# Edge counting in a four-layer graph transformer: the check of the totals, the node normalization, the bias rows and a register load change their places

## The chip, the core and the metric

The kernel runs on one core of one Trainium2 chip. The metric is device time in microseconds (us) of one execution. Below, PE is the TensorE matmul engine (PEld its weight loads), DVE is VectorE, ACT is ScalarE, POOL is GpSimd, SP is the queue that starts most transfers. A "q" behind the name (PEldq, DVEq) is the engine's own queue of control instructions.

## What is computed

The reference is one forward pass through four layers on 512 nodes with 768 features. Each layer adds a graph network, a mixture (attention) and a feed-forward network to the nodes. Only the beginning matters here:

```python
xn = _layernorm(x, axis=-1)
x = x + _L0_gnn_ref(xn, edge_index, edge_attr_256, ...) + _L0_mix_ref(xn[None], ...)[0]
...
def _L0_mix_ref(x, qkv_w, qkv_b, proj_w, proj_b, rf):
    qkv = x @ qkv_w.T + qkv_b
    ...
    phi_q = jnp.exp(jnp.einsum('bhnd,md->bhnm', q, rf) - q_norm)
    ...
    return out @ proj_w.T + proj_b
```

There are 8704 edges, with a source, a destination, two type numbers and 256 attributes each. The graph networks need, for each pair of nodes, how many edges of each type join them, and for each node the sum of the attributes of its edges.

## The kernel before

The four layers follow one another in one program of some 39000 instructions. A scheduler puts the instructions of each engine into one fixed order when the program is built: of those that it takes to be ready, the one that stands first in the program goes first. At run time each engine works through its own queue in that order, and an instruction that waits holds up all that is queued behind it. `tc.issue_after(ins)` adds only this: what is written in its block for the engine of `ins` is queued behind `ins`. A tile that lies where an earlier, closed pool lay can be written only when the tiles there have been read for the last time.

**Counting** (`counts`, L431). The edges lie as 128 rows of 68. For each of the 68 columns DVE builds a one-hot matrix of destinations (`ohd`, L510, kept for all 68) and a pair of one-hot matrices of sources, weighted by powers of 256 for the types (`so`, L513, four buffers); PE adds up their products in four PSUM banks (L516). This runs twice, over the lower and the upper 256 source nodes (`h` = 0, 1). Between the columns, every fourth time, the edge attributes of two columns are split into three bf16 parts (L466 to L469, ACT and DVE by turns) and added up over the destinations (L474). After each half, `digits` takes the sums apart: DVE reads the banks (L485), ACT turns bytes into numbers (L488 into `S`, L490 into `R`), POOL and DVE add them up (L492 to L498), ACT and POOL send three results to memory. `S` and `R` have one buffer each, so the second use of `S` waits for the transfer of the first. `eft` holds the attribute sums in two more banks until they are copied to `EFT` (L250, L252). There are eight banks in all (L180).

**The check** (L530 to L544). Type numbers above 2, sums that don't fit, or totals that differ set a flag, `big`. DVE reduces the totals, PE adds them over the partitions (a 128 x 128 matrix of ones by `check`), and DVE makes the flag from it. It is written at the end of `counts`.

**Nodes.** `norm` (L391 to L406) takes statistics (L402, L403) and a root (L404, L405) for each of four blocks of 128 nodes and scales them into `xn` (L406). It is queued behind column 34 of the second half (`begun`). `to_fm` (L357) turns `xn` with 24 transposes on PE (L355) into six banks, and six copies bring them into `xnT` (DVE and ACT by turns). `xn` and `xnT` are in pools opened behind `counts`, on the memory of the counting.

**First mixture** (`mix0`, L644). `tm` (L319) multiplies `xnT` by the weights of the values in eight groups of twelve matmuls and a thirteenth that adds the bias; then come two groups of four heads, and `project`, which turns the result and multiplies it by the output weights, again with a bias row. `bias` (L280) fetches one row of 768 numbers with POOL's queue and splits it into three bf16 parts with five POOL instructions: three copies (L291, L293, L295) and two subtractions (L292, L294).

**Branches.** Behind the mixture each of the five engines loads the flag into a register (L2089) and takes a branch (L2090); with a flag of 0 the longer counting is skipped. The third layer does the same again (L1560, L1561).

Of the kernel before, what the change touches and what calls it, by code (L numbers as in the profile page):

```python
# [10 lines left out]
F32 = mybir.dt.float32  # L11
BF16 = mybir.dt.bfloat16
# [4 lines left out]
OP = mybir.AluOpType  # L17
# [4 lines left out]
P = 128  # L22
N = 512
NT = N // P
D = 768
KC = D // P
HW = 384
NE = 8704
EJ = NE // P
# [141 lines left out]
class Net:  # L171
    def __init__(self, ctx, tc, dram, at, out):
# [43 lines left out]
        nc.gpsimd.iota(self.me, pattern=[[0, 1]], base=0, channel_multiplier=1, allow_small_or_imprecise_dtypes=True)  # L216
        self.identb = keep.tile([P, P], BF16, name="identb")
        self.big0 = keep.tile([P, 1], F32, name="big0")
        nc.gpsimd.memset(self.big0, -BIG)
# [211 lines left out]
    def counts(self, c0, g0):  # L431
# [10 lines left out]
        AT = g0.tile([P, NT, N], F32, name="AT")  # L442
        after = c0.enter_context(tc.tile_pool(name="g0_t", bufs=1))
        EFT = after.tile([P, 2, N], F32, name="EFT")
        with ExitStack() as c:
# [10 lines left out]

            top = one.tile([P, 8], F32, name="top")
            total = one.tile([P, 10], F32, name="total")

# [19 lines left out]
            def digits(h, t, ps):  # L479
# [8 lines left out]
                nc.scalar.copy(S[:, :3, :], held[0])  # L488
                R = dg.tile([P, 3, N], F32, name="R", bufs=1)
                nc.scalar.copy(R, held[1])  # L490
                R16 = dg.tile([P, 3, N], I16, name="R16", bufs=1)
                nc.gpsimd.tensor_copy(R16, R)  # L492
                nc.gpsimd.tensor_add(A, R[:, 0, :], R[:, 1, :])
                nc.vector.scalar_tensor_tensor(A, A, 0.0, R[:, 2, :], OP.add, OP.add, accum_out=total[:, k : k + 1])
# [11 lines left out]
            for h in range(2):  # L506
# [15 lines left out]
                for t in range(2):  # L522
                    digits(h, t, [acc[t, n] for n in range(2)])

                while len(left) > (17, 0)[h]:
                    features(left.pop(0))
            for f in range(2):
                self.copy(EFT[:, f, :], eft[f])

            three = one.tile([P, EJ], F32, name="three")  # L530
            nc.vector.tensor_scalar(three, ind[:, 3, :], 2.0, None, OP.is_le, OP.add, accum_out=total[:, 8:9])
            nc.vector.tensor_scalar(total[:, 8:9], total[:, 8:9], -1.0, float(-EJ), OP.mult, OP.add)
            nc.vector.memset(total[:, 9:10], 0.0)
            check = one.tile([P, 2], F32, name="check")
            nc.vector.tensor_reduce(check[:, 0:1], total, AX.X, OP.add)
            high = one.tile([P, 1], F32, name="high")
            nc.vector.tensor_reduce(high, top, AX.X, OP.max)
            nc.vector.tensor_scalar(check[:, 1:2], high, 2.0 ** 24, None, OP.is_ge)
            p = self.ps()
            self.acc(p[:, :2], [(self.ones, check)])  # L540
            bad = one.tile([P, 2], F32, name="bad")
            nc.vector.tensor_scalar(bad, p[:, :2], 0.0, None, OP.not_equal)
            nc.vector.tensor_reduce(high, bad, AX.X, OP.max)
            nc.vector.tensor_copy(self.big, high)  # L544
        return AT, EFT, after

# [96 lines left out]

    def mix0(self, xnT):  # L644
        nc, tc, d = self.nc, self.tc, self.d
        scale = 96 ** -0.5
        xs = self.chunks(xnT)
        with ExitStack() as outer, ExitStack() as c:
# [15 lines left out]

            self.tm(d["m0_wqkv"], xs, put_v, self.bias(d["m0_bv"]), nbs=(4, 5), bias_at=2 * D)
            for g in range(2):
                qk = one.tile([97, 2, 4, N], F32, name="qk")
                for s, b in ((0, "m0_bq"), (1, "m0_bk")):
# [47 lines left out]
            c.close()  # L716
            self.project(outer, attn, "m0")

# [840 lines left out]
    def gnn2(self, xn, xnT):  # L1559
        big = self.nc.values_load(self.big[:1], min_val=0, max_val=1)  # L1560
        with self.tc.If(big > 0) as cmp:  # L1561
            self.gnn2_with(xn, xnT, False)
        with cmp.Else():
            self.gnn2_with(xn, xnT, True)
# [497 lines left out]
def tile_net(ctx, tc, dram, at, out, only=ALL):  # L2062
# [10 lines left out]
    with ExitStack() as ck, ExitStack() as c0:  # L2073
        g0 = c0.enter_context(tc.tile_pool(name="g0", bufs=1))
        if "counts" in only:
            AT, EFT, g0_t = net.counts(c0, g0)
        nodesT = ck.enter_context(tc.tile_pool(name="L0k", bufs=1, side="right")).tile([P, KC, N], F32, name="nodesT")
        with tc.tile_pool(name="L0", bufs=1) as pool:
            xnT = pool.tile([P, KC, N], F32, name="xnT")
            with tc.tile_pool(name="L0n", bufs=1) as p2:  # L2080
                xn = p2.tile([P, NT, D], F32, name="xn")
                with tc.issue_after(net.begun[0]), tc.issue_after(net.begun[1]):
                    net.constants()
                    net.norm(net.x, xn)
                net.to_fm(xn, xnT)
            if "mix0" in only:
                net.mix0(xnT)
            if "gnn0" in only:
                wrong = nc.values_load(net.big[:1], min_val=0, max_val=1)  # L2089
                with tc.If(wrong > 0):  # L2090
                    net.counts_any(AT)
                with ExitStack() as e:
                    net.gnn0(nodesT, xnT, AT, net.degrees(e, g0_t, AT, EFT))
        c0.close()
        if "gnn0" in only:
            net.attention0(nodesT)
# [62 lines left out]
```

## Time and profile before

| | us |
|---|---|
| median of three runs (4174.07 to 4178.53) | 4176.57 |
| the profiled execution | 4179.75 |
| its span | 4177.7 |
| PE busy | 4027.0 (96%) |
| first matmul of the counting | 13.24 |
| end of the first half's matmuls of columns | about 119 |
| first matmul of the second half | 127.5 |
| flag written (L544) | 246.2 |
| first matmul of the mixture's values | 252.36 |
| first matmul behind the branch | 489.63 |

A row of the timeline reads: start and duration in us, engine, line, operation, what is written <- what is read, shape, number of instructions merged, and in brackets the idle time of the engine before it with what ended it. A row of the waits reads: who waited <- for what, then total us, number of times, longest. "Granted clock" is the share of full speed at which TensorE was let run in a stretch. All spans come from one profiled execution.

### The profile page before, as it was taken

How to read it: one execution, taken by the hardware profiler on the slowest of the kernel's cores; microseconds unless marked ns; L12 is line 12 of the kernel's file. 1: busy time of each engine (PE TensorE's matmuls, PEld its weight loads, DVE VectorE, ACT ScalarE, POOL GpSimd, SP SyncE). 2: the span in 40 equal slices, each digit the busy share in tenths (PEclk: the TensorE clock that was granted, in tenths of full speed). 3: DMA queues.
4: the chain of work that ended last, by engine and by line, in shares of the span. 5: the costliest groups of instructions: out<-in, count | busy, mean ns of one | idle time of the engine just before them, and what ended most of it. 6: DMA issues, size and time to landing. Idle time of an engine off the chain costs nothing. (4 is left out here: it accounts for less than half of the span.)

```text
span 4177.7 us, 39229 instructions
## 1 busy us (share of the span) xinstructions
PE 4027.0 (96%) x16020; PEld 2066.7 (49%) x16061; DVE 1214.8 (29%) x2899; ACT 648.5 (16%) x1222; POOL 274.4 (7%) x329
## 2 busy tenths in 40 slices
PE   8989999999999999999999999999989999999998
PEld 3444555554455667655544444454644444444443
DVE  7721211113332147313411111126832122212211
ACT  1212000012222216311101010024510000000000
POOL 1120000010031010000000000020200000000000
PEclk9999999999999999999999999999999999999999
DMA  3210011121184011302211111082099999999998
GB/s 124 71 69 34 35 63 51 53 78 36 62 312 143 23 70 46 132 25 78 98 46 57 46 61 42 3 325 82 15 373 422 421 421 421 421 422 421 422 422 361
DMA packets 99548, 710.89 MB, mean 170 GB/s; under 512 B 12608, under 2 KB 12944, under 8 KB 29984
## 3 DMA queue, kind: packets, MB, share of 16 engines
q1 hardware_dynamic: 78064, 601.20, 36.0%
q0 software_dynamic: 16816, 95.80, 6.1%
q10 hardware_dynamic: 4480, 11.28, 0.7%
q8 instruction: 131, 2.15, 0.2%
q14 instruction: 57, 0.47, 0.0%
HBM read 685.68 MB, written 22.54 MB: 170 GB/s over the span
## 5 line engine op out<-in xcount | busy, mean ns | idle before, releaser
L1981 PE MATMUL ps<-w,xg 128*64 128x384 f32 x3072 | 567.6, 489 | 5.3 <-DMA w<-in_f_Wg_dram 3.0
L1981 PEld LDWEIGHTS ps<-w,xg 128*64 128x64 f32 x3072 | 235.3, 137 | 293.1 <-issue 264.1
L1601 PE MATMUL ps<-aT,w 128*128 128x512 f32 x864 | 372.3, 592 | 0.0
L1997 PE MATMUL ps<-w,hT 128*64 128x384 f32 x1536 | 322.5, 490 | 6.3 <-DMA w<-in_f_Wd_dram 2.9
L334 PE MATMUL ps<-xnT,w 128*128 128x512 f32 (+1 forms) x732 | 322.8, 598 | 0.2 <-ACT xnT L252 0.2
L1601 PEld LDWEIGHTS ps<-aT,w 128*128 128x128 f32 x864 | 164.2, 190 | 203.6 <-issue 202.3
L334 PE MATMUL ps<-w,xnT 128*128 128x384 f32 x672 | 222.7, 488 | 0.0
L334 PEld LDWEIGHTS ps<-xnT,w 128*128 128x128 f32 (+1 forms) x732 | 134.7, 185 | 176.3 <-issue 172.7
L1997 PEld LDWEIGHTS ps<-w,hT 128*64 128x64 f32 x1536 | 132.5, 136 | 171.8 <-issue 146.5
L411 DVE TENSOR_TENSOR x<-x,ps 128x384 f32<-128x384 f32 x224 | 123.4, 553 | 263.7 <-PE ps L334 193.0
L334 PE MATMUL ps<-C,parts 128*128 128x512 bf16 x843 | 187.8, 380 | 3.5 <-DVE inv L1623 2.4
L334 PE MATMUL ps<-w,hT 128*128 128x384 f32 x552 | 184.6, 490 | 2.6 <-ACTq L1056 1.7
L334 PEld LDWEIGHTS ps<-w,xnT 128*128 128x128 f32 x672 | 127.7, 191 | 88.8 <-issue 5.8
L1611 DVE TENSOR_TENSOR aT<-inv,ps 128x512 f32<-128x512 f32 x72 | 49.4, 686 | 365.7 <-PE ps L334 365.7
L1984 ACT ACTIVATE h<-ps 128x384 f32<-128x384 f32 x64 | 31.4, 490 | 788.9 <-PE ps L1981 788.9
L516 PE MATMUL ps<-ohd,so 128*128 128x512 bf16 x533 | 128.4, 391 | 21.1 <-DVE so L513 20.4
L1985 DVE TENSOR_TENSOR h<-h,ps 128x384 f32<-128x384 f32 x64 | 35.4, 554 | 376.8 <-PE ps L1981 376.8
L334 PEld LDWEIGHTS ps<-w,hT 128*128 128x128 f32 x552 | 103.1, 190 | 80.1 <-ACT xbT L252 7.1
L334 PE MATMUL ps<-w,aT 128*128 128x384 f32 (+1 forms) x416 | 139.6, 486 | 0.5 <-DVE aT L250 0.4
L334 PE MATMUL ps<-xnT,sw 128*128 128x512 f32 x288 | 139.6, 616 | 0.0
L334 PEld LDWEIGHTS <-parts 128*128 128x128 bf16 x864 | 84.8, 98 | 108.1 <-issue 8.9
L334 PE MATMUL ps<-w,nodesT 128*128 128x384 f32 x384 | 129.1, 486 | 0.0
(507 smaller groups left out, 4634.7 us busy)
## 6 DMA issues: line engine op xcount, KB each, us to landing
w<-in_f_Wg_dram SPq DMA_DIRECT2D x128, 1152.0 KB, 22.2
w<-in_f_Wu_dram SPq DMA_DIRECT2D x128, 1152.0 KB, 22.2
w<-in_f_Wd_dram SPq DMA_DIRECT2D x128, 1152.0 KB, 22.2
w<-in_g_w_dram SPq DMA_DIRECT2D x54, 1152.0 KB, 5.2
w<-in_m_wqkv_dram SPq DMA_DIRECT2D x24, 1152.0 KB, 7.5
w<-in_g_t_dram SPq DMA_DIRECT2D x12, 1152.0 KB, 5.1
w<-in_m_wp_dram SPq DMA_DIRECT2D x8, 1152.0 KB, 5.1
ea<-in_edge_attr_dram SPq DMA_DIRECT2D x34, 256.0 KB, 2.7
```

Source lines behind the costliest of these rows:

```text
L334: i = self.nc.tensor.matmul(out, a, b, start=n == 0, stop=n == len(pairs) - 1)
L411: self.nc.vector.tensor_add(xs, xs, p)
L516: nc.tensor.matmul(p, so[:, n, t * P : (t + 1) * P], ohd[:, j, :], start=j == 0, stop=j == EJ - 1)
L1601: nc.tensor.matmul(outs[nb * 3 + f], w[:, k, f * P : (f + 1) * P], xT[:, k, :], start=first and k == 0, stop=last and k == KC - 1)
L1611: nc.vector.tensor_mul(aT[:, f, :], inv[:, r, :], p)
L1981: nc.tensor.matmul(p[a * 64 : a * 64 + 64, :HW], xg[:, k, a * CAP : (a + 1) * CAP], ws[b][a][:, k, :], start=k == 0, stop=k == KC - 1)
L1984: nc.scalar.activation(h, pg[:, :HW], AF.Silu)
L1985: nc.vector.tensor_mul(h, h, pu[:, :HW])
L1997: nc.tensor.matmul(po[nb][a * 64 : a * 64 + 64, :HW], hT[:, f * P + a * 64 : f * P + a * 64 + 64], wd[a][:, f, nb * HW : (nb + 1) * HW], s ...
```

## The change

Six things are altered.

- The small tiles of the check move into one long-lived tile, `edge`. The check itself becomes a function, `checked`, that `mix0` calls behind the products of the values. The counting of type numbers (L531 to L533) is queued behind column 34 of the second half.
- `xn` is allocated before the counting, on the right side of the memory, in a place of its own; normalization is otherwise queued as before. `nodesT` takes that place once `xn` has been turned. `EFT` is allocated behind the counting instead of before it.
- `R` is bf16 instead of f32.
- The bias row of the values and all of POOL's work in `project` are queued behind the last POOL sum of counts of the first half (`self.after`, L493 with `t` = 1). At the start of the program they were free to go at once.
- The flag is loaded once, ahead of the second group of heads, and both branches use that register.
- The third layer's load is dropped.

```diff
--- before.py
+++ after.py
@@ -215,6 +215,7 @@
         self.me = keep.tile([P, 1], F32, name="me")
         nc.gpsimd.iota(self.me, pattern=[[0, 1]], base=0, channel_multiplier=1, allow_small_or_imprecise_dtypes=True)
         self.identb = keep.tile([P, P], BF16, name="identb")
+        self.edge = keep.tile([P, 24], F32, name="edge")
         self.big0 = keep.tile([P, 1], F32, name="big0")
         nc.gpsimd.memset(self.big0, -BIG)
         self.wq1 = keep.tile([P, KC, 32], F32, name="wq1")
@@ -440,8 +441,6 @@
         self.S32 = self.dp.tile([NT, P, 4, N], F32, name="S32")
         self.big = self.keep.tile([P, 1], I32, name="big")
         AT = g0.tile([P, NT, N], F32, name="AT")
-        after = c0.enter_context(tc.tile_pool(name="g0_t", bufs=1))
-        EFT = after.tile([P, 2, N], F32, name="EFT")
         with ExitStack() as c:
             one = c.enter_context(tc.tile_pool(name="c_one", bufs=1))
             ep = c.enter_context(tc.tile_pool(name="c_e", bufs=2))
@@ -454,8 +453,7 @@
             attr = d["edge_attr_256"].rearrange("(p j) f -> p j f", p=P)
             eft = [self.ps() for _ in range(2)]
 
-            top = one.tile([P, 8], F32, name="top")
-            total = one.tile([P, 10], F32, name="total")
+            top, total, check, high, bad = (self.edge[:, a:b] for a, b in ((0, 8), (8, 18), (18, 20), (20, 21), (21, 23)))
 
             def features(q):
 
@@ -486,11 +484,12 @@
                     held.append(whole.bitcast(U8).rearrange("p (n b) -> p b n", b=4)[:, :3, :])
                 S = dg.tile([P, 4, N], F32, name="S", bufs=1)
                 nc.scalar.copy(S[:, :3, :], held[0])
-                R = dg.tile([P, 3, N], F32, name="R", bufs=1)
+
+                R = dg.tile([P, 3, N], BF16, name="R", bufs=1)
                 nc.scalar.copy(R, held[1])
                 R16 = dg.tile([P, 3, N], I16, name="R16", bufs=1)
                 nc.gpsimd.tensor_copy(R16, R)
-                nc.gpsimd.tensor_add(A, R[:, 0, :], R[:, 1, :])
+                made["add"] = nc.gpsimd.tensor_add(A, R[:, 0, :], R[:, 1, :])
                 nc.vector.scalar_tensor_tensor(A, A, 0.0, R[:, 2, :], OP.add, OP.add, accum_out=total[:, k : k + 1])
                 nc.gpsimd.tensor_add(S[:, 3, :], S[:, 0, :], S[:, 1, :])
                 nc.vector.scalar_tensor_tensor(S[:, 3, :], S[:, 3, :], 0.0, S[:, 2, :], OP.add, OP.add,
@@ -521,28 +520,34 @@
                         self.begun = made["so"].ins, made["part"].ins
                 for t in range(2):
                     digits(h, t, [acc[t, n] for n in range(2)])
+                if h == 0:
+                    self.after = made["add"].ins
 
                 while len(left) > (17, 0)[h]:
                     features(left.pop(0))
-            for f in range(2):
-                self.copy(EFT[:, f, :], eft[f])
 
             three = one.tile([P, EJ], F32, name="three")
-            nc.vector.tensor_scalar(three, ind[:, 3, :], 2.0, None, OP.is_le, OP.add, accum_out=total[:, 8:9])
-            nc.vector.tensor_scalar(total[:, 8:9], total[:, 8:9], -1.0, float(-EJ), OP.mult, OP.add)
-            nc.vector.memset(total[:, 9:10], 0.0)
-            check = one.tile([P, 2], F32, name="check")
+            with tc.issue_after(self.begun[0]):
+                nc.vector.tensor_scalar(three, ind[:, 3, :], 2.0, None, OP.is_le, OP.add, accum_out=total[:, 8:9])
+                nc.vector.tensor_scalar(total[:, 8:9], total[:, 8:9], -1.0, float(-EJ), OP.mult, OP.add)
+                nc.vector.memset(total[:, 9:10], 0.0)
+        after = c0.enter_context(tc.tile_pool(name="g0_t", bufs=1))
+        EFT = after.tile([P, 2, N], F32, name="EFT")
+        for f in range(2):
+            self.copy(EFT[:, f, :], eft[f])
+
+        def checked():
+
             nc.vector.tensor_reduce(check[:, 0:1], total, AX.X, OP.add)
-            high = one.tile([P, 1], F32, name="high")
             nc.vector.tensor_reduce(high, top, AX.X, OP.max)
             nc.vector.tensor_scalar(check[:, 1:2], high, 2.0 ** 24, None, OP.is_ge)
             p = self.ps()
             self.acc(p[:, :2], [(self.ones, check)])
-            bad = one.tile([P, 2], F32, name="bad")
             nc.vector.tensor_scalar(bad, p[:, :2], 0.0, None, OP.not_equal)
             nc.vector.tensor_reduce(high, bad, AX.X, OP.max)
             nc.vector.tensor_copy(self.big, high)
-        return AT, EFT, after
+
+        return AT, EFT, after, checked
 
     def counts_any(self, AT):
 
@@ -641,7 +646,7 @@
         return EFP
 
 
-    def mix0(self, xnT):
+    def mix0(self, xnT, checked):
         nc, tc, d = self.nc, self.tc, self.d
         scale = 96 ** -0.5
         xs = self.chunks(xnT)
@@ -662,8 +667,13 @@
                 h = (nb - 4) * 4
                 self.copy(v[:, t, h : h + 4, :96], p.rearrange("p (h d) -> p h d", h=4))
 
-            self.tm(d["m0_wqkv"], xs, put_v, self.bias(d["m0_bv"]), nbs=(4, 5), bias_at=2 * D)
+            with tc.issue_after(self.after):
+                bv = self.bias(d["m0_bv"])
+            self.tm(d["m0_wqkv"], xs, put_v, bv, nbs=(4, 5), bias_at=2 * D)
+            checked()
             for g in range(2):
+                if g:
+                    self.wrong = nc.values_load(self.big[:1], min_val=0, max_val=1)
                 qk = one.tile([97, 2, 4, N], F32, name="qk")
                 for s, b in ((0, "m0_bq"), (1, "m0_bk")):
                     w = self.wk(d["m0_wqkv"][2 * s + g, 0])
@@ -714,7 +724,8 @@
                     nc.vector.tensor_mul(attn[:, :, hh * 96 : (hh + 1) * 96], p[:, :, :96],
                                          r.to_broadcast([P, NT, 96]))
             c.close()
-            self.project(outer, attn, "m0")
+            with tc.issue_after(self.after):
+                self.project(outer, attn, "m0")
 
     def project(self, c, attn, m, done=None):
 
@@ -1557,8 +1568,7 @@
             self.project(c, attn, "m2")
 
     def gnn2(self, xn, xnT):
-        big = self.nc.values_load(self.big[:1], min_val=0, max_val=1)
-        with self.tc.If(big > 0) as cmp:
+        with self.tc.If(self.wrong > 0) as cmp:
             self.gnn2_with(xn, xnT, False)
         with cmp.Else():
             self.gnn2_with(xn, xnT, True)
@@ -2073,21 +2083,21 @@
     with ExitStack() as ck, ExitStack() as c0:
         g0 = c0.enter_context(tc.tile_pool(name="g0", bufs=1))
         if "counts" in only:
-            AT, EFT, g0_t = net.counts(c0, g0)
-        nodesT = ck.enter_context(tc.tile_pool(name="L0k", bufs=1, side="right")).tile([P, KC, N], F32, name="nodesT")
+            right = ExitStack()
+            xn = right.enter_context(tc.tile_pool(name="L0n", bufs=1, side="right")).tile([P, NT, D], F32, name="xn")
+            AT, EFT, g0_t, checked = net.counts(c0, g0)
+            with tc.issue_after(net.begun[0]), tc.issue_after(net.begun[1]):
+                net.constants()
+                net.norm(net.x, xn)
         with tc.tile_pool(name="L0", bufs=1) as pool:
             xnT = pool.tile([P, KC, N], F32, name="xnT")
-            with tc.tile_pool(name="L0n", bufs=1) as p2:
-                xn = p2.tile([P, NT, D], F32, name="xn")
-                with tc.issue_after(net.begun[0]), tc.issue_after(net.begun[1]):
-                    net.constants()
-                    net.norm(net.x, xn)
-                net.to_fm(xn, xnT)
+            net.to_fm(xn, xnT)
+            right.close()
+            nodesT = ck.enter_context(tc.tile_pool(name="L0k", bufs=1, side="right")).tile([P, KC, N], F32, name="nodesT")
             if "mix0" in only:
-                net.mix0(xnT)
+                net.mix0(xnT, checked)
             if "gnn0" in only:
-                wrong = nc.values_load(net.big[:1], min_val=0, max_val=1)
-                with tc.If(wrong > 0):
+                with tc.If(net.wrong > 0):
                     net.counts_any(AT)
                 with ExitStack() as e:
                     net.gnn0(nodesT, xnT, AT, net.degrees(e, g0_t, AT, EFT))
```

## The prediction

> **What bounds the kernel now.** I read the busy shares first. TensorE (PE) is busy 96% of a span of 4177.7 us, so a change pays only where PE stands still or runs at a low clock. The edit touches the counting of the edges and the first mixture, all before 500 us. Next I read the waits of PE from 0 to 560 us.
>
> ```profile
> PE ps L516 <- DVE so L513: 20.4, 8, 13.2
> PE ps L334 <- DVE check L535: 7.8, 1, 7.8
> PE ps L334 <- DVEq L2090: 6.2, 1, 6.2
> ...
> PE ps L474 <- ACT part L468: 2.9, 2, 2.2
> ```
>
> Columns: total us, times, longest. The first row holds 13.2 us of start-up; the remaining 7.2 us are short of one-hot pairs (`so`) at the start and between the two halves of the counting. The second is the test of the totals, the third the branch behind the mixture. Then the timeline of PE at the start, and of DVE and POOL beside it.
>
> ```profile
> 13.24 3.90 PE L516 MATMUL ps<-ohd,so 128*128 128x512 bf16 x9 [13.24 <-DVE so L513]
> 17.53 0.82 PE L516 MATMUL ps<-ohd,so 128*128 128x512 bf16 x3 [0.38 <-DVE so L513]
> 19.94 0.40 PE L516 MATMUL ps<-ohd,so 128*128 128x512 bf16 x1 [1.59 <-DVE so L513]
> 21.64 3.17 PE L516 MATMUL ps<-ohd,so 128*128 128x512 bf16 x7 [1.30 <-DVE so L513]
> 26.57 8.10 PE L516 MATMUL ps<-ohd,so 128*128 128x512 bf16 x28 [1.76 <-DVE so L513]
> ```
>
> ```profile
> 14.97 2.50 DVE L513 TENSOR_SCALAR so<-io,ind,worth 128x256 bf16<-128x256 int16 x2
> 14.98 1.63 POOL L292 TENSOR_TENSOR row<-row,bias 1x768 f32<-1x768 f32 x1
> ```
>
> Nine matmuls in 3.90 us are 0.43 each; the three at 17.53 take 0.27. So PE comes up to its full clock after about 3.9 us of unbroken work, loses it in the gaps (granted clock 0.50 from 20 to 30 us), and has it again at 30.4. The gaps come from DVE: the same pair of `so` takes 0.59 us at 12.85 and 2.50 at 14.97, while POOL splits bias rows. Last, the end of the counting:
>
> ```profile
> 235.54 1.90 PE L474 MATMUL ps<-ohd,part 128*128 128x512 bf16 x7 [1.21 <-DVE part L469]
> 245.25 0.56 PE L334 MATMUL ps<-check,ones 128*128 128x2 f32 x2 [7.81 <-DVE check L535]
> 247.24 5.27 PE L355 MATMUL ps<-ident,xn 128*128 128x128 f32 x24 [1.43 <-DVE xn L406]
> 252.36 4.11 PE L334 MATMUL ps<-w,xnT 128*128 128x384 f32 x12
> ```
>
> PE ends the edge features at about 237.3, waits for the check, then for the normalized nodes, turns them at half clock (0.50 from 242 to 252) and starts the mixture's values at 252.36: 15.1 us.
>
> **The change, part by part.**
>
> *Bias rows away from the start.* Two rows, `m0_bv` and `m0_bp`, cost POOL three copies of 0.81 and two subtractions of 1.63 each: 5.69 a row, 11.4 us, from 13.99 to 26.43. In that time (14.13 to 25.63) DVE finished twelve operations worth 0.26 each, 3.1 us of work in 11.5: 27%. It isn't the DMA traffic: the DMA engines were full already at 12.6 to 14.0, where `ohd` took its normal 0.34. Without the rows DVE makes one edge column in 0.26 + 2 x 0.26 = 0.78 us; PE uses one in 4 x 0.226 = 0.90 (sixteen matmuls in 3.62 us at full clock) or 1.72 cold. So PE is never starved after 13.24: nine cold matmuls to 17.14, then 39 at 0.226 = 8.8, so the first feature group, which starts at 34.51 now, starts at 26.0. **-8.5**. Bounds: -5.0, the gaps alone (0.38 + 1.59 + 1.30 + 1.76), and -9. I take -8.5, since the three matmuls at 17.53 were at full clock.
>
> *The rows in their new place.* They are queued on POOL behind the last sum of counts of the first half (L493, now at 131.3) and ahead of, or among, L495, L498 and three transfers of the digits; their two row fetches (0.53 each to issue) go with them, and the rows of the first graph layer, fetched at 22 and 26 now, come after. Queued behind POOL are DVE's L496, which waits for L495, and every `so` behind that. The same 11.4 us of POOL now lie at about 136 to 150. DVE loses 73% of them, 8.3 us. It is what PE waits for until 141; afterwards it stands idle 2.5 us of each 6.05:
>
> ```profile
> 146.15 0.69 DVE L467 TENSOR_TENSOR ea<-ea,part 128x512 f32<-128x512 f32 x1 [2.50 <-ACT part L466]
> ```
>
> Two such pauses give back 5.0, so 3.3 stay. **+3.3**, bounds 0 (four `so` buffers cover it) and +8.3 (nothing does). Here a rule of the Trainium skill speaks against the change: SBUF — State Buffer (the summary of port contention) says that DVE in its two-port modes and GpSimd hold a port pair in turn, each blocking the other for a whole instruction. By the rule alone moving a row moves its whole block: 11.4 away, 11.4 back, nothing won. The rows say DVE does get 27% through, and that the price depends on DVE's slack at the place: 8.5 where it has none and the clock is cold, 3.3 where it idles 41%.
>
> *Nodes normalized beside the counting.* Statistics and roots already run at 174 to 183; only the four scalings (L406, 2.52 us) waited, as their tile lay in memory that the counting held. On the other side of SBUF they can run at 183. The DVE queue holds `so` behind them; DVE idles 2.5 of the next 6 us and features are prepared one group ahead. **0**; without that cover +2.5. Below nothing: no, DVE work is only added there.
>
> *The end of the counting.* The check leaves the path, and with `xn` ready the 24 transposes follow the features at 237.3. At full clock the same step is in the trace at the mixture's end:
>
> ```profile
> 447.53 2.97 PE L355 MATMUL ps<-ident,attn 128*128 128x128 f32 x24
> 450.91 4.14 PE L334 MATMUL ps<-w,aT 128*128 128x384 f32 x12 [0.41 <-DVE aT L250]
> ```
>
> 3.4 us from first transpose to next projection. They need six PSUM banks: two are free in the second half, and four are read out by L485 until 231.7. The copies to `xnT` share DVE and ACT with the last digits: I add 0.6, one such operation. The values start at 241.3 instead of 252.36. **-11.1**. Bounds: -8, if the copies queue behind L488 and L500, which wait for the digits' transfer and end at 243.4; -13, if transposes fill PE's two gaps of 1.9 us at 233 to 236. The clock: TensorE: Matmul & The Clock Gate (the HAM part) has the gate close after one idle window of about 3.4 us. By that alone PE, only half busy from 232 to 238, might meet the transposes cold: 5.27 instead of 2.97, -8.8. The row gives 1.00 until 242, 4.7 us after PE stopped, and 1.00 through the similar gaps at 132 to 142. I use the row.
>
> *The check inside the mixture.* Its three DVE steps, one product, and three DVE steps (0.15 each) go behind the values. On PE it costs 0.56 for two passes cold, about half warm: **+0.3** (bounds 0 and 1). DVE waits for PE mostly there (7.5 us at a time). The counting of types (L531 to L533) moves off DVE's start, which waits for a transfer at that point: 0.
>
> *bf16 digits.* R shrinks; ACT writes it, POOL and DVE read it. The nearest rows, POOL's copies of one row from f32 and from bf16, both take 0.81: 0, bounds -1 and +2 (four sums of 1.3 us).
>
> *One register load.* Each engine now loads the flag at the second head group, about 366 us. On PE's queue it takes 0.487 at 477.8 while matmuls go on to 483.5, so it hides behind queued matmuls (2.03 us of them before 366): 0, bounds 0 and +1.5. What waits behind it: PE's next projection, ACT's exponentials, DVE's scalings. SP's load must wait for the flag at about 275; the projection's weights may queue behind it and are used at 440. At the branch, DVE's load of 0.55 (483.5) goes and the branch itself stays: **-0.5** (0 to -0.6). The later loads, at 2033 on PE, made nobody wait: 0.
>
> Sum: -8.5 + 3.3 + 0 - 11.1 + 0.3 - 0.5 = -16.5. The profiled execution took 4179.75 us (2.05 more than its span); it would take 4163.3. The runs shown have a median of 4176.57, 3.2 lower, so: **4160**. Everything behind 500 us, the last stage's weight stream included, shifts as a whole.
>
> **Rivals.**
> *The covers hold too well or the rows cost nothing:* transposes fill the gaps, DVE hides the rows: -8.5 - 13 - 0.2 = -21.7, 4155.
> *The rows cost all that DVE loses:* -8.5 + 8.3 - 11.1 - 0.2 = -11.5, 4165. For it: DVE is behind when they come. Against: the pauses at 144 and 150.
> *The rows do not thin out the start, or the copies queue behind the digits:* the scheduler orders DVE anew and the start stays starved (-11.1 + 3.3 - 0.2 = -8), or the full loss and late copies together (-8.5 + 8.3 - 8 - 0.2 = -8.4): 4168.5, near to no change.
> *DVE's queue stands in the middle (slower):* L496 is queued ahead of the pairs, at 133, and POOL splits both rows before L495. The row fetches land as late as the first did (7.5 us from issue to first use), at 141; then 11.4 of rows and 1.5 of L495: DVE stands until 154, 21 us, PE runs dry and restarts cold (half of 3.9 us, 1.9): +22.9 in place of +3.3, a sum of +3.1, 4180. It decides from 20 us on. Against it: L496 comes late in DVE's queue now (138.93), behind five pairs, and the same order should follow POOL's new one.
>
> **How the numbers follow.** Forecast (4156 to 4164) 0.52; covers too good 0.13; full price 0.14; near no change 0.14; slower 0.07. A measurement here can't tell less than 0.2%, 8.4 us. Faster by over that: the first three nearly whole, 0.77; slower by over that: the tail of the last, 0.03; between, 0.20. The range 4153 to 4170 takes in the fourth case and leaves out the slower one and the far end of the second.
>
> **What would show it.** First feature group near 26; PE without gaps at 17 to 27. POOL's row steps (L291 to L295) behind the first half's digits, and DVE's pairs slow beside them; PE's waits for `so` there up by 3. L406 before 190. Transposes near 232 in 3.0 us (all is 5.2 earlier by then: -8.5 + 3.3), values 4 us after their start. The branch's wait 5.7. It would be wrong if the row steps fell beside another late DVE stretch, or if the transposes waited for a place, a bank or the clock.

## The result and the profile after

The changed kernel took 4162.06 us (median of nine runs, 4156.76 to 4168.25), the kernel before 4178.16 on the same chip (nine runs, 4174.07 to 4181.6): ratio 0.9962, 95% interval 0.9952 to 0.9972, 16.1 us less. The forecast was 4160 from a median of 4176.57, a step of 16.5. The terms of the sum did not all come out so well: the rows cost half of what was forecast in their new place, the register load won nothing, and a loss of 3.1 us stood in no term.

The profiled execution took 4156.76 us for a span of 4154.5. The views of before are taken up in their order. The waits of PE from 0 to 560 us (who waited <- for what: total us, times, longest):

```profile
PE ps L515 <- DVE so L512: 15.4, 5, 11.9
PE ps L335 <- DVEq L2100: 6.5, 1, 6.5
...
PE ps L472 <- ACT part L466: 2.8, 2, 1.7
```

The wait of 7.8 us for the check is gone. The wait for one-hot pairs is down by 5.0, the branch's wait is there as before. The timeline of PE and of DVE at the start:

```profile
11.94 13.08 PE L515 MATMUL ps<-ohd,so 128*128 128x512 bf16 x48 [11.94 <-DVE so L512]
24.86 2.75 PE L472 MATMUL ps<-ohd,part 128*128 128x512 bf16 x12
```

```profile
15.95 0.60 DVE L512 TENSOR_SCALAR so<-io,ind,worth 128x256 bf16<-128x256 int16 x2
```

48 matmuls run without a break, and a pair of `so` takes 0.60 us at about the time at which it took 2.50 before. The first group of edge attributes starts at 24.86; the forecast said 26.0. Behind the first half's digits PE waited for pairs before, too (first fence); now POOL's row steps lie there, and the waits are longer (second fence, PE and then DVE beside it):

```profile
133.49 3.27 PE L516 MATMUL ps<-ohd,so 128*128 128x512 bf16 x12 [0.55 <-DVE so L513]
138.04 2.76 PE L516 MATMUL ps<-ohd,so 128*128 128x512 bf16 x12 [1.28 <-DVE so L513]
```

```profile
128.15 4.44 PE L515 MATMUL ps<-ohd,so 128*128 128x512 bf16 x19 [1.34 <-DVE so L512]
139.55 0.82 PE L515 MATMUL ps<-ohd,so 128*128 128x512 bf16 x3 [1.31 <-DVE so L512]
130.16 9.34 DVE L512 TENSOR_SCALAR so<-io,ind,worth 128x256 bf16<-128x256 int16 x10
```

The end of the counting, on PE:

```profile
227.68 1.90 PE L472 MATMUL ps<-ohd,part 128*128 128x512 bf16 x8 [0.21 <-DVE part L467]
229.42 2.78 PE L356 MATMUL ps<-ident,xn 128*128 128x128 f32 x24
232.49 4.11 PE L335 MATMUL ps<-w,xnT 128*128 128x384 f32 x12 [0.29 <-ACT xnT L253]
```

The transposes follow the last attributes with nothing between, at full clock (2.78 us for 24), and the values start at 232.49 instead of 252.36.

All comparisons below use three distances, all between first matmuls on PE: *start* (first column to first group of attributes), *half 2* (last group of attributes in the first half to last group in the second), *tail* (from there to the mixture's values). The changed kernel was profiled twice (experiment 10), and the two executions differ in their clock.

| kernel | first matmul | start | half 2 | tail | values start | median us (before on that chip) |
|---|---|---|---|---|---|---|
| before | 13.24 | 21.27 | 108.15 | 25.09 | 252.36 | |
| changed | 11.94 | 12.92 | 109.87 | 13.15 | 232.49 | 4162.06 (4178.16) |
| changed, second profile | 11.98 | 13.05 | 109.82 | 13.14 | 232.60 | 4163.53 (4177.14) |
| rows early | 12.12 | 22.02 | 107.93 | 12.97 | 239.64 | 4166.59 (4174.07) |
| rows only | 13.06 | 11.96 | 110.05 | 25.29 | 244.97 | 4166.86 (4174.07) |
| check first | 12.21 | 12.35 | 109.81 | 23.54 | 242.52 | 4167.05 (4174.07) |
| nodes late | 12.87 | 13.20 | 109.82 | 18.15 | 238.64 | 4161.64 (4174.07) |
| `edge` 64 wide | 11.43 | 12.25 | 109.82 | 14.69 | 232.79 | 4158.84 (4176.66) |
| pad in before | 11.68 | 20.82 | 108.15 | 25.11 | 250.37 | 4179.33 (4176.66) |
| rows in an idle place | 12.00 | 12.46 | 110.14 | 15.12 | 234.32 | 4161.74 (4176.66) |
| two loads | 13.01 | 12.43 | 109.85 | 14.82 | 234.72 | 4162.59 (4176.66) |
| rows spread | 11.96 | 12.59 | 108.57 | 13.13 | 230.85 | 4158.28 (4177.14) |

The medians of one kernel before differ by up to 4 us between chips, so a median is read against the one in brackets beside it.

### The profile page after: what moved, and what is told of

Read it like the earlier page. It is cut to its first block, busy times and chain, and to the rows that moved or that the text cites. A ratio compares the mean times of both kernels' runs of the same rounds, so it can differ in the third digit from the quotient of the medians.

```text
span 4154.5 us, 39257 instructions
## 1 busy us (share of the span) xinstructions
PE 4020.7 (97%) x16061; PEld 2061.7 (50%) x16061; DVE 1212.8 (29%) x2899; ACT 648.6 (16%) x1222; POOL 273.4 (7%) x329
```

## The experiments

**1. Rows early.** The changed kernel with the bias rows free to go at once, as they were.

```
-            with tc.issue_after(self.after):
-                bv = self.bias(d["m0_bv"])
+            bv = self.bias(d["m0_bv"])
...
-            with tc.issue_after(self.after):
-                self.project(outer, attn, "m0")
+            self.project(outer, attn, "m0")
```

> The changed kernel with both bias rows free to go at the start again, as before the change; all else as changed. Theory (POOL's row steps starve DVE at the start, and cost less behind the first half's digits): the first feature group is back near 33 to 34.5 us instead of 24.9, the step between the halves is as short as in the kernel before, the tail is as short as in the changed kernel; values of the mixture start near 240 (before 252.4, changed 232.5), total about 12 us below the kernel before and 6 to 8 above the changed one. Rival (the transfers, not POOL, starve DVE at the start): first feature group stays near 25 and the total equals the changed kernel's.

Measured 4166.59, ratio 0.9982 (0.9973 to 0.9991). PE at the start:

```profile
22.98 1.89 PE L515 MATMUL ps<-ohd,so 128*128 128x512 bf16 x4 [2.21 <-DVE so L512]
...
34.14 2.75 PE L472 MATMUL ps<-ohd,part 128*128 128x512 bf16 x11
```

The gaps are back and the attributes start at 34.14, with everything else of the change in place: POOL's row steps, and nothing else that was altered, thinned the start. (Their two small fetches move with them; experiment 7 has the same thinning with the DMA engines 14% busy.) Between the halves this kernel takes 107.93, as before (108.15). Its matrix of normalized nodes is made within that stretch (179.3 to 186.8), so the four scalings cost nothing there. The total missed its expectation: 7.5 us below the kernel before instead of 12. The values do start 12.7 earlier, but 3.2 of that is lost in the last stage (experiments 5 and 6) and 1.1 is the first matmul's, which no part of the change explains.

**2. Rows only.** The kernel before with that one part of the change.

```
-                nc.gpsimd.tensor_add(A, R[:, 0, :], R[:, 1, :])
+                made["add"] = nc.gpsimd.tensor_add(A, R[:, 0, :], R[:, 1, :])
...
+                if h == 0:
+                    self.after = made["add"].ins
...
+            with tc.issue_after(self.after):
+                bv = self.bias(d["m0_bv"])
...
+            with tc.issue_after(self.after):
+                self.project(outer, attn, "m0")
```

> The kernel before with nothing changed but the place of the two bias rows. Theory: first feature group near 25 to 26, between the halves 2 to 3.5 us lost again, tail of 15.1 us as before: values start near 244.5 to 247, total 5 to 8 us below the kernel before. Rival (a move of the rows wins nothing, since their whole block comes back): total within 2 us of the kernel before, with PE's waits for pairs between the halves up by 8.

Measured 4166.86, ratio 0.9984 (0.9977 to 0.9991): 7.2 us less, where experiment 1, all but this part, gave 7.5 less. Start 11.96, 9.3 shorter; between the halves 110.05, 1.9 longer; tail unchanged. So the rows are worth 8 to 9 at the start and cost about 2 where they go.

**3. Check first.** The changed kernel, with the transposes held behind the check; the nodes are still ready early.

```
-            self.acc(p[:, :2], [(self.ones, check)])
+            self.checking = self.acc(p[:, :2], [(self.ones, check)]).ins
...
-            checked()
...
-            net.to_fm(xn, xnT)
+            checked()
+            with tc.issue_after(net.checking):
+                net.to_fm(xn, xnT)
```

> The changed kernel with the check called right behind the counting, and the transposes queued behind its product on PE. Theory (the wait for the check was most of the tail, and cost the clock as well): PE stands about 8 us for the check, the transposes take 5.3 us at half clock instead of 2.8, values start about 10.5 us later than in the changed kernel (243), total up by 10 to 11 against it. Rival (nodes ready early is what counted, the check would be hidden by it): values start within 3 us of the changed kernel's.

Measured 4167.05, ratio 0.9986 (0.9979 to 0.9992). PE at the end of the counting:

```profile
237.09 0.56 PE L335 MATMUL ps<-edge,ones 128*128 128x2 f32 x2 [6.70 <-DVE edge L541]
237.50 4.78 PE L356 MATMUL ps<-ident,xn 128*128 128x128 f32 x24
242.52 4.14 PE L335 MATMUL ps<-w,xnT 128*128 128x384 f32 x12 [0.24 <-DVE xnT L251]
```

The tail is 23.54. Ready nodes alone are worth only 1.6 of the 11.9 us: PE waits 6.70 for the totals, and then turns the nodes at about half speed, 4.78 instead of 2.78.

**4. Nodes late.** The changed kernel, with `xn` back in the memory of the counting and the check left in the mixture.

```
-            right = ExitStack()
-            xn = right.enter_context(tc.tile_pool(name="L0n", bufs=1, side="right")).tile([P, NT, D], F32, name="xn")
...
-            net.to_fm(xn, xnT)
-            right.close()
...
+            with tc.tile_pool(name="L0n", bufs=1) as p2:
+                xn = p2.tile([P, NT, D], F32, name="xn")
+                with tc.issue_after(net.begun[0]), tc.issue_after(net.begun[1]):
+                    net.constants()
+                    net.norm(net.x, xn)
+                net.to_fm(xn, xnT)
```

> The changed kernel with the normalized nodes back in the memory that the counting gives free; the check stays in the mixture. Theory: the four scalings start only behind the last feature matmul, transposes begin 0.7 to 1.5 us later and keep full clock; values start 1 to 2.5 us later than in the changed kernel, total up by as much. Rival (the own place was the larger part): values start 5 us later or more.

Measured 4161.64, ratio 0.9970 (0.9958 to 0.9982); tail 18.15, 6.9 shorter than before. The three views are PE, DVE and POOL at the end of the counting:

```profile
234.09 4.26 PE L356 MATMUL ps<-ident,xn 128*128 128x128 f32 x24 [3.37 <-DVE xn L407]
```

```profile
231.37 4.41 DVE L407 TENSOR_SCALAR xn<-x,mv,rs 128x768 f32<-128x768 f32 x4
```

```profile
230.93 1.48 POOL L491 CAST R<-R 128x1536 int16<-128x1536 bf16 x1
232.36 1.16 POOL L492 TENSOR_TENSOR AT<-R 128x512 f32<-128x512 bf16 x1
```

The expectation missed: the tail is 5.0 longer than the changed kernel's, not 1 to 2.5, and the transposes did not keep full clock. The four scalings took 4.41 us here and 2.52 in the kernel before: they now lie beside POOL's digits, the same collision as at the start. Moving the check alone gives 6.9, early nodes alone 1.6, both 11.9. The two parts are worth 3.4 more together than one by one: each alone leaves PE a wait (6.70 or 3.37), and behind it slow transposes (4.78 or 4.26).

**5 and 6. The tile `edge`.** The profile of the changed kernel showed a loss that no step of the forecast had: from the first down product of the last stage to the end 1080.4 us, where the kernel before and experiment 2 have 1077.3. Experiments 1, 3 and 4 are as slow (1080.3 to 1080.5). What all the slower ones have and the other two have not includes `edge`, 96 bytes per partition that live to the end; every tile allocated behind it, the weight buffers included, lies 96 bytes further on. Experiment 5 gives it 256 bytes in the changed kernel; experiment 6 adds 96 bytes to the kernel before, and changes nothing else.

```
-        self.edge = keep.tile([P, 24], F32, name="edge")
+        self.edge = keep.tile([P, 64], F32, name="edge")
```

```
+        pad = keep.tile([P, 24], F32, name="pad")
+        nc.gpsimd.memset(pad, 0.0)
```

> The changed kernel with the long-lived tile of the check 256 bytes wide instead of 96, so that all that lies behind it in SBUF stands where it stood before, modulo 256. Theory (the 96 bytes shift the last stage's weight buffers off a 256-byte boundary, and each 9216-byte piece of a transfer then takes 351 ns instead of 349): pieces back at 349 ns, rate back at 422 GB/s, from the first down product of the last stage (near 3070) to the end 1077.3 us as before instead of 1080.4, total 3 us below the changed kernel, near 4159. Rival (the last stage is longer for its later or earlier start or the missing register load): still 1080.4, 351 ns.

> The kernel before with an unused long-lived tile of 96 bytes and nothing else. Theory: pieces of 9216 bytes take 351 ns, the last stage 1080.4 us instead of 1077.3, values start as before (252), total 3 us above the kernel before. Rival: no change.

Measured 4158.84, ratio 0.9957 (0.9944 to 0.9971), and 4179.33, ratio 1.0007 (0.9999 to 1.0015). The last stage took 1077.1 in the first and 1080.4 in the second, and the pieces of 9216 bytes took 349 and 351 ns. Medians alone would not settle it, as the interval of experiment 6 just touches 1; the windows from 3700 to 3900 us do, in the order before, changed, experiment 5, experiment 6. The columns are the window, its length, busy time (and number) of PE, PEld, DVE, ACT and POOL, granted clock, DMA share and, last, GB/s.

```profile
3700.00:3900.00 200.00, 199.38 (x1034) 89.34 (x1032) 38.24 (x102) 11.95 (x24) 4.24 (x7) 1.00 1.01 422
```

```profile
3700.00:3900.00 200.00, 197.81 (x999) 87.22 (x996) 45.26 (x129) 11.47 (x23) 4.24 (x7) 1.00 1.01 420
```

```profile
3700.00:3900.00 200.00, 199.28 (x1017) 88.38 (x1014) 44.14 (x126) 11.50 (x23) 4.24 (x7) 1.00 1.01 421
```

```profile
3700.00:3900.00 200.00, 198.53 (x1022) 88.42 (x1018) 39.42 (x108) 11.98 (x24) 4.24 (x7) 1.00 1.01 420
```

The DMA engines are full in all four, and with the 96 bytes they move less. The waits of PE in the last stage (3070 to the end) show whom it reaches, first before, then changed:

```profile
PE ps L1981 <- DMA w<-in_f_Wg_dram: 3.0, 2, 1.5
PE ps L1997 <- DMA w<-in_f_Wd_dram: 2.9, 5, 1.2
```

```profile
PE ps L2007 <- DMA w<-in_f_Wd_dram: 3.9, 5, 1.2
PE ps L1991 <- DMA w<-in_f_Wg_dram: 3.8, 3, 1.5
```

These rows hold 1.8 of the 3.1 us; the rest stands in no row of PE's waits. The stage waits for its weights, so it has no slack for a slower stream.

**7. Rows in an idle place.** Experiment 5 with the rows behind column 24 of the second half, where DVE has pauses in each group.

```
+                    if h == 1 and j == 24:
+                        tiny = self.edge[:1, 23:24]
+                        self.after = nc.gpsimd.tensor_copy(tiny, so[:1, 0, :1]).ins
...
-                if h == 0:
-                    self.after = made["add"].ins
```

> The changed kernel with the 256-byte tile, and with the bias rows queued behind column 24 of the second half (through a one-element copy on POOL), where DVE idles. Theory (the rows cost 1.9 us between the halves since DVE is behind there): PE's waits for pairs behind the rows vanish, values start near 230.6, 1.9 us earlier than in the changed kernel, total 5 below it, near 4157. Rival (the rows cost as much wherever DVE works): values start at 232.5 again, or up to 5 later if the pairs run out in steady counting.

Measured 4161.74, ratio 0.9960 (0.9947 to 0.9974). Between the halves it takes 110.14, no less than in the crowded place: the rival, not the theory. (The values start at 234.32, but 2.0 of that is a half-clock stretch in the tail.) POOL's row steps lie from 150.98 to 163.75; DVE's operations on `so` alone, ahead of and beside them, and then PE:

```profile
139.00:151.00 12.00, 4.39 (x17) 1.00 0.16 46
151.00:163.70 12.70, 8.54 (x8) 1.00 0.14 42
```

```profile
161.31 0.39 PE L515 MATMUL ps<-ohd,so 128*128 128x512 bf16 x1 [0.37 <-DVE so L512]
163.02 1.95 PE L515 MATMUL ps<-ohd,so 128*128 128x512 bf16 x7 [1.32 <-DVE so L512]
```

Seventeen `so` operations in 12 us (0.26 each) become eight in 12.7 (1.07 each). PE lives on the four buffers for ten microseconds and then stands 0.37 and 1.32. Single operations show how DVE is slowed (DVE and POOL side by side, twice):

```profile
157.23 1.78 DVE L512 TENSOR_SCALAR so<-io,ind,worth 128x256 bf16<-128x256 int16 x1
157.30 1.63 POOL L295 TENSOR_TENSOR bias<-row,mid 1x768 bf16<-1x768 f32 x1
161.18 1.79 DVE L512 TENSOR_SCALAR so<-io,ind,worth 128x256 bf16<-128x256 int16 x1
161.25 1.63 POOL L295 TENSOR_TENSOR bias<-row,mid 1x768 bf16<-1x768 f32 x1
```

Each `so` ends 0.08 or 0.09 us behind the POOL step beside it, and so does each of the seven that start from 154 to 163: DVE gets one `so` through for each step of POOL. The wait of 1.32 is for the second of these.

**8. Two loads.** The changed kernel with a register load ahead of each branch, as before.

```
-                if g:
-                    self.wrong = nc.values_load(self.big[:1], min_val=0, max_val=1)
...
-        with self.tc.If(self.wrong > 0) as cmp:
+        big = self.nc.values_load(self.big[:1], min_val=0, max_val=1)
+        with self.tc.If(big > 0) as cmp:
...
-                with tc.If(net.wrong > 0):
+                wrong = nc.values_load(net.big[:1], min_val=0, max_val=1)
+                with tc.If(wrong > 0):
```

> The changed kernel with the flag loaded twice again, each time ahead of its branch. Theory (the single load stands where the first stood, so nothing was won or lost): loads of PE, DVE, ACT and POOL again just ahead of the branch, branch wait 6.2 to 6.5, total within 1 us of the changed kernel's. Rival (the single load won the 0.5 us that the forecast gave it): total 0.5 or more above it, with the branch's wait up by 0.5.

Measured 4162.59, ratio 0.9963 (0.9950 to 0.9977), the changed kernel's own 0.9962. Where the single load of the changed kernel really stands is told by its line (L676; duration least/median/most in ns, first and last start in us):

```profile
L676 ACTq TENSOR_LOAD <-big x1: 467/467/467, 430.9 to 430.9; - x1
L676 PEldq TENSOR_LOAD <-big x1: 488/488/488, 458.1 to 458.1; - x1
L676 POOLq TENSOR_LOAD <-big x1: 497/497/497, 463.8 to 463.8; - x1
L676 DVEq TENSOR_LOAD <-big x1: 553/553/553, 463.8 to 463.8; - x1
```

On these four engines it still stands behind the mixture: the values start 19.9 us earlier than before, and these loads 19.6 to 19.7 (450.5, 477.8, 483.5 and 483.5 before). SP alone loads the flag early, right behind its writing, and it did so before (246.4, and 265.7 now). Only the second set, behind 1890 us, is gone, and nobody had waited for it.

**9. Rows spread.** Experiment 5, with each of the ten row steps queued behind another column of the second half (8, 12 and so on to 44), so that POOL works for one step at a time.

```
+                    if h == 1 and j in (8, 12, 16, 20, 24, 28, 32, 36, 40, 44):
+                        self.slots.append(nc.gpsimd.tensor_copy(self.edge[:1, 23:24], so[:1, 0, :1]).ins)
...
+            with tc.issue_after(self.slots[0]):
+                bv = self.bias(d["m0_bv"], slots=self.slots[:5])
...
+                    with self.tc.issue_after(slots.pop(0)):
+                        fn(*args)
```

> The changed kernel with the 256-byte tile, and with the ten POOL steps of the two bias rows let go one by one, each behind another column of the second half (every fourth from 8 to 44). Theory (a row costs what DVE loses beyond its idle time in the same 6 us; one step of at most 1.63 takes 1.2 us of DVE, against 2.5 idle): no waits for pairs beside the row steps, counting from the first half's last features to the second's (109.9 in the changed kernel, 107.9 with the rows at the start) back to 108; values start near 230.6, total about 5 below the changed kernel, 4157. Rival (a fixed cost of some 2 us wherever the rows lie): 110 again, values at 232.5.

Measured 4158.28, ratio 0.9954 (0.9940 to 0.9968). Between the halves it takes 108.57, 0.4 more than before and 0.6 more than with the rows early. From 151 to 163.7 us:

```profile
151.00:163.70 12.70, 12.65 (x60) 5.77 (x59) 8.31 (x21) 3.76 (x5) 3.07 (x4) 1.00 0.14 42
```

PE is busy for all of it. POOL has 3.07 us of work there, where experiment 7 had 12.29, and DVE finishes 21 operations, where experiment 7 had 10.

**10. The changed kernel again**, for a second profile beside experiment 9.

> The changed kernel once more, on the chip of the spread rows, for a second profile. Theory (early gain of 19 to 20 us up to the mixture's values, 3 us given back in the last stage): values start at 232 to 234, last stage 1080.4 us from its first down product, total 4160 to 4164. Rival (the first profile's 4154.5 us span is what the change gives): span again under 4156.

Measured 4163.53, ratio 0.9964 (0.9952 to 0.9977); profiled execution 4163.84, 7.1 us longer than the first. All the distances of the table agree within 0.15. The difference lies where the change does not reach, as the window from 1334 to 1346 us shows (first profile, then second):

```profile
1334.00:1346.00 12.00, 11.16 (x74) 9.60 (x74) 1.82 (x7) 2.98 (x7) 0.00 (x0) 1.00 0.01 1
```

```profile
1334.00:1346.00 12.00, 11.13 (x46) 8.54 (x45) 0.76 (x3) 4.41 (x9) 0.00 (x0) 0.72 0.12 51
```

The granted clock is 1.00 in one and 0.72 in the other. Such stretches at half clock, here and at 1267, cost the second profile 5.1 of the 7 us (it is 0.7 behind the first ahead of them and 5.8 behind them). The kernel before has them too (at 1287 and 1358), so the second profile is the one to set beside it.

## Why the prediction was right, point by point

The account from the second profile against that of before: first matmul -1.3, start -8.2, rest of the first half 0, half 2 +1.7, tail -11.9, the mixture and its branch +0.4, the last stage +3.1. Between the branch and the last stage nothing changes (2606.5 us in both). With the first matmul that is -16.2; the medians differ by 16.1. That two single executions agree so well with medians that scatter over 7.5 and 11.5 us is in part luck, and so is the closeness to the forecast: it was 0.3 too hopeful for the start, 1.6 and 0.8 too careful for the rows and the tail, 0.6 too hopeful for the check and the branch together, and left out the last stage's +3.1 and the first matmul's -1.3.

- **Rows away from the start, -8.5: right.** -8.2 to -8.4 in the changed kernel, -9.3 alone, and experiment 1 gives it all back. The sum took 3.9 us for PE to come up to its clock; that varies, and the start with it, from 11.96 to 13.20 in the nine profiles without rows there.
- **Rows in their new place, +3.3: right mechanism, wrong size and a wrong reason.** It cost 1.7 to 2.0. The forecast counted as lost all that DVE could have done beside the rows (8.3), set it against DVE's pauses at the place and took 5.0 back. Experiment 7 put the rows where DVE has such pauses all the time, and they cost as much. What counts is what DVE must deliver meanwhile: beside the unbroken run of POOL steps it finished 10 operations where it finishes 21 beside thin ones, the deficit grows with the length of the run, and the buffers cover the first ten microseconds. Experiment 9 does the same POOL work one step at a time and pays 0.4. The forecast also set the Trainium skill's rule (SBUF — State Buffer, the summary of port contention) against the rows, as if it gave back a whole block of 11.4. That was a misreading: the rule speaks of single instructions, each blocked until the other's ends, and one `so` for each POOL step, as experiment 7 has it, is what it describes (for operations in a two-port mode; whether `so` is one, the rows don't say). The 27% are no exception to it. A step let go alone holds up one operation: beside one of 1.74 in experiment 9 four `so` take 2.43 us instead of 1.10.
- **Nodes normalized beside the counting, 0: right** (experiment 1, 107.93 against 108.15). In the changed kernel the scalings start at 172.0 to 179.5.
- **The end of the counting, -11.1: right**, -11.9. Experiments 3 and 4 show that it needs both edits. On the clock the forecast used the row (1.00) against the rule in TensorE: Matmul & The Clock Gate (the HAM part), and the changed kernel's two profiles had the clock. It was not safe. Experiments 5, 7 and 8 have the same code there, and in them a half-clock stretch of 3.4 us fell into the tail, which was 14.7 to 15.1 long: a part of what the forecast feared came true, 1.6 to 2.0 us. Experiments 2, 3 and 6 had one there too, ahead of the check's wait. PE of experiment 5:

```profile
226.31 1.78 PE L472 MATMUL ps<-ohd,part 128*128 128x512 bf16 x5 [1.09 <-DVE part L467]
228.31 1.06 PE L472 MATMUL ps<-ohd,part 128*128 128x512 bf16 x2 [0.22 <-issue]
229.16 3.34 PE L356 MATMUL ps<-ident,xn 128*128 128x128 f32 x24
```

  Two matmuls take 1.06 us, where eight take 1.90 in the changed kernel, and the transposes 3.34 instead of 2.78. PE is never idle for a whole 3.4 us here, so the rule's one idle window does not describe it either; PE stands in gaps of 0.7 and 1.1. Windows of experiment 5, then of the changed kernel (columns as in experiments 5 and 6):

```profile
223.50:226.90 3.40, 1.57 (x7) 0.42 (x6) 1.93 (x6) 1.84 (x3) 3.10 (x3) 1.00 0.28 114
226.90:230.30 3.40, 3.18 (x12) 1.97 (x11) 0.69 (x1) 1.36 (x2) 3.40 (x5) 0.50 0.50 199
```

```profile
225.40:228.80 3.40, 1.73 (x8) 0.65 (x9) 2.19 (x6) 2.37 (x3) 2.42 (x4) 1.00 0.29 116
228.80:232.20 3.40, 3.40 (x28) 2.85 (x26) 1.20 (x2) 1.23 (x3) 3.40 (x4) 1.00 0.68 270
```

  In every profile the half-clock stretches start on one grid of 3.41 us (within 0.03). In the lightest window of that grid beside these last attributes PE was busy for 34 to 47% in the six profiles that got the stretch, and for about 50% or more in the other six, a narrow margin. So the stretch goes with where the grid happens to lie, and that the changed kernel's two profiles had full clock was luck. No run moved the grid by itself, and this is no threshold for other places: experiment 4 has a window of 1.45 busy us of 3.40 at 2885.8, with full clock behind it.
- **The check in the mixture, +0.3: right.** The step between the groups around it is 0.31 us in the changed kernel and 0.17 before, +0.14.
- **bf16 digits, 0: right as far as the rows show.** At the end of the counting ACT writes `R` in 1.47 us before and after, POOL's copy takes 1.48 both times, POOL's sum 1.27 and 1.16, DVE's 0.69 and 0.68. The changed kernel with `R` in f32 was not tried.
- **One register load, -0.5: the step failed** where it said "each engine now loads the flag at the second head group". So nothing was won. The place in the program is not the place in the queue: the scheduler had put the loads of PE, ACT, DVE and POOL behind the mixture, at the branch, as before. The wait there is 6.4 to 6.5 us against 6.2, and 6.2 with two loads.
- **The tile `edge`: not priced.** The forecast held that the last stage "shifts as a whole". It did not: its weight stream was slower by half a per cent, 3.1 us, shown by taking the shift out (experiment 5) and by putting it in alone (experiment 6). The total came out right because the stretch up to the values gained 19.8 instead of 16.3, and this took 3.1 of it back. Of these 19.8, 1.3 are the first matmul's. It stands behind the first attributes on DVE and these behind their transfer, and varies from 11.4 to 13.2 between kernels with no order that follows the change (12.12 with early rows, 13.06 with late rows alone, 11.68 in experiment 6).

None of the rivals took place as written. The slower one, DVE's queue stopped in the middle, did not: PE's longest wait for pairs between the halves is 1.34 us in the first profile and 1.53 in the second.

**A better version** of both is experiment 9. Beside the second run of the changed kernel on the same chip it is 5.2 us lower (4158.28 against 4163.53); the intervals of the two overlap (0.9940 to 0.9968, 0.9952 to 0.9977), but the profiles show where 4.9 of it lie: 1.75 at the start of the values and 3.1 in the last stage.

## What to carry to other kernels

Price work that is moved beside another engine by what the slowed engine must deliver meanwhile, by how many of its operations get through (here one for each step of the other), and by the buffers between them: an unbroken run of 12.7 us cost as much in an idle place as in a busy one, and nearly nothing in single steps. A new tile that lives long moves everything behind it: ask which transfers land there, and whether a stage that waits for them has slack. Look up in the queue, not in the program, where a load or a wait will stand.

## What the runs showed of the hardware that was not expected

- **A shift of 96 bytes slows a DMA stream.** The pieces of 9216 bytes in which weights arrive took 351 ns (median) with it and 349 without. In DMA: Bandwidth & Descriptors (How a descriptor splits into AXI transactions) the Trainium skill counts pieces of 256 bytes that start at multiples of 256; by that a piece shifted by 96 bytes would need 37 transactions instead of 36, but only 291 beats of 32 bytes instead of 288, an estimate of 1.0% more, if it held for the side that is written, which the section doesn't say. The runs show 0.6%, and that 256 bytes bring the speed back. Other offsets weren't tried, so that 256 is the unit is not shown.
- **Stretches at half clock last multiples of 3.4 us** (3.4, 6.8, 10.2, 13.7 and 17.1 were seen) and start on one grid in each execution, and whether a given light place gets one differs between two executions of one kernel. Much of the spread of some 10 us between its runs may come from this; it was traced for one pair of profiles only.
- **Beside an unbroken run on POOL, DVE gets one one-hot operation through for each POOL step.** That leaves it about a quarter of its speed, at the start of the kernel before (27%) and at 151 us in experiment 7 (0.26 us becomes 1.07), where the DMA engines are 14% busy. The quarter is the ratio of these operations to these steps (0.81 to 1.63 us), and not a fixed share.
